# Which queue issues the transfers of the later stages, and three smaller edits, in a four-layer convolution kernel

## The chip, the cores and the metric

The kernel runs on one core of a Trainium2 chip, in one launch. The metric is the device time of that launch in microseconds (us), the median of three runs. A core has five engines that run side by side, each with its own instruction queue that it works through in order: TensorE (PE; its weight loads are shown as PEld), VectorE (DVE), ScalarE (ACT), GpSimd (POOL) and SyncE (SP). Engines wait for each other, and for transfers between memory and the core, by semaphores. A transfer is issued by an instruction in the queue of one engine; the instruction stands in that queue until what it waits for has happened.

## The reference

Four layers follow each other on x with 16 images, 32 channels and 128 x 128 points, each with a normalisation over pairs of channels before it and a residual sum after it:

```python
x = x + _L0_conv_ref(_gn(x), ...)   # a recurrence along the image's columns
x = x + _L1_conv_ref(_gn(x), ...)   # 3x3 sum of absolute differences, quantised
x = x + _L2_conv_ref(_gn(x), ...)   # Hartley transform, 32 x 32 modes mixed, transform back
x = x + _L3_conv_ref(_gn(x), ...)   # five edge operators, then a small encoder and decoder
```

The second layer is the long one. For each image, each output channel f and each point it computes

```python
out[n, f, i, j] = -sum over c, kh, kw of |patch[c, kh, kw] - w[f, c, kh, kw]|
```

with integers in patch and w. The fourth layer has convolutions on 128, 64, 32 and 16 points a side, max pooling between them, and three 2 x 2 deconvolutions back up; its output multiplies its input.

## The kernel before

**First layer** (`stage0`). It runs alone at the start and isn't touched.

**Absolute differences** (`Differences`). The work is cut into 32 units: 16 images by 2 halves of 64 rows. A unit loads its quantised half image once (`loaded`, tile `q`, 128 partitions of 4 channel copies) and makes 72 evaluations, one for each of 8 filter blocks and 9 taps. An evaluation is one instruction over the half image, max(q - w, 0): either on VectorE (L684, tile `d_dve`, three buffers) or on ScalarE (L681, tile `d_act`, two buffers). Each evaluation is summed over the channels by 16 pairs of a weight load and a matmul (`sums`, L586) into four PSUM banks (`acc`); nine `linear` steps add the part of the absolute value that max leaves out. At the end `finish` (L567, L569) adds the residual on VectorE and takes statistics, and stores the rows (L573). Its own transfers are the quantised store (L546), the unit's load (L553), the residual (L560) and the rows to be quantised next (L530).

**Later stages** (`After`). The third and fourth layers run for groups of four images, so there are four groups. Groups 0 to 2 are woven into the units, as soon as their images are finished; group 3 and what is left of group 2 run after the last unit. Before all groups, `prepare` composes weights and stores them in memory (`up`, `fold`). In a group, `forward` loads the images (`xh`, L961), transforms them, stores the modes (`xm_d`, L1010), loads them again in two orders (`xs` and `xw`, L1061) and mixes them with weights (`mix`, L1083; result `z_d`, L1120). `back` loads that (`zi`, L1145), transforms back and adds the residual (`xr`, L1138), and stores x3 (L1188). `frames` loads x3 in strips of rows (`xp`, L1246), which `statistics` (matmuls L1292) and `conv1` (matmuls L1607) read. `small_layers` does the convolutions (L1455) and deconvolutions (`round`, L822 and L847) with `spread` (L1543 on VectorE, L1546 on ScalarE) writing their results, and `last` the final one, with a last store of the output (L1714).

**What sets the order.** Python code plans the order of instructions while the program is built. `Weave` keeps estimated clocks for TensorE, VectorE and ScalarE (`weave.pe`, `weave.dve`, `weave.act`; an evaluation counts 2.36 on VectorE and 7.15 on ScalarE). `Differences.run` asks which engine would finish the next evaluation first, with its buffers taken into account, emits it there, emits sums whose evaluations should be done, and lets `weave.advance` fill in steps of the later stages where TensorE should have room. Steps with `later(us, ...)` are put off by that many planned microseconds: a store comes some us after its computation, a load some us after the store that frees its tile. `keep_order` then ties each engine to this order while the units run. After the last unit `drain` takes turns between two such workers, the rest of group 2 and group 3, each with its own four PSUM banks (`b_ps` and `c_ps`). Nothing on the chip adapts: an instruction that is late holds up what stands behind it on its engine.

Two details matter for the change. A unit's last evaluations were kept from ScalarE, and all its sums were emitted before the next unit's first evaluation:

```python
act = False not in ends or (True in ends and i < 68 and ends[True] <= ends[False] + 0.5)
...
if acc and (not act or i == 71):
    sums(weave.dve, i == 71)
```

And all transfers after the start, of the differences and of the later stages alike, are issued by SyncE (1321 of them; ScalarE issues three at the start, GpSimd none). GpSimd has a few memsets only (L519, L952, L953, L1255) and one reduction.

Of the kernel before, what the change touches and what calls it, by code (L numbers as in the profile page):

```python
# [7 lines left out]
F32 = mybir.dt.float32  # L8
# [8 lines left out]
HW = H * W  # L17
# [282 lines left out]
class Weave:  # L300
# [10 lines left out]
    def __init__(self, work):  # L311
# [3 lines left out]
        self.draining = False  # L315
# [87 lines left out]
def drain(*weaves):  # L403
# [4 lines left out]
    while live:  # L408
# [4 lines left out]
        if us is None:  # L413
            live.remove(w)

# [17 lines left out]
DVE_US, ACT_US, PE_US = 2.36, 7.15, 1.0  # L433
SLACK, CLOCK = 3.0, 1.0
# [3 lines left out]
def rest(nc, tc, cst, sel16, bias, m1, r1, a, d, out):  # L438


    with ExitStack() as ctx:
# [13 lines left out]
        end.side, end.ps = "right", ctx.enter_context(tc.tile_pool(name="c_ps", bufs=4, space=PSUM))  # L455
        end.weave = Weave(end.work([NG - 1]))
# [5 lines left out]
class Differences:  # L462
# [100 lines left out]
    def finish(self, b, half, acc, xr):  # L563
# [46 lines left out]
    def run(self, tc, ctx, weave):  # L610
# [13 lines left out]
        before, following = None, self.loaded(0, 0)  # L624

        free, count = {True: [0.0] * 2, False: [0.0] * 3}, {True: 0, False: 0}
        for b in range(B):
            for half in range(2):
                q, acc = following, None
                late, xq, summed = [], {}, 0  # L630

                def sums(until, last):

                    nonlocal summed
                    while late and (min(late)[0] <= until or last):
                        end, n, act, t = min(late)
                        late.remove((end, n, act, t))
                        self.sums(acc, t, n, not summed, last and not late)
                        summed += 1
                        weave.pe = max(weave.pe, end + 0.2) + PE_US  # L640
                        free[act].append(weave.pe)

                for i in range(72):
                    if not acc and sum(not v[2] for v in late) == 2:

                        if before:
                            self.finish(*before)
                        acc = [ps.tile([128, 512], F32, name="acc1") for _ in range(4)]
                        sums(weave.dve, False)
                    if i % 4 == 0 and 24 <= i < 60:  # L650
                        self.linear(acc, q, i // 4 - 6)
                    if i == 8 and (b, half) != (B - 1, 1):
                        following = self.loaded(b + half, 1 - half)
                    if i == 40:
                        xr = self.residual(b, half)
# [17 lines left out]
                    act = False not in ends or (True in ends and i < 68 and ends[True] <= ends[False] + 0.5)  # L673
# [4 lines left out]
                    late.append((ends[act], i, act, t))  # L678
# [7 lines left out]
                    if acc and (not act or i == 71):  # L686
# [1227 lines left out]
```

## Time and profile before

| | us |
|---|---|
| median of three runs (7311.98 to 7319.36) | 7317.06 |
| the profiled execution | 7308.39 |
| its span, in the trace | 7306.6 |
| TensorE busy | 5566.3 (76%) |
| VectorE busy | 5855.4 (80%) |
| ScalarE busy | 5318.0 (73%) |
| GpSimd busy | 36.3 |
| mean granted clock of TensorE | 0.867 |

The span runs from the first to the last instruction of one execution; the 1.8 us around it are not in the trace. Busy shares over the whole span mix three stages: the first layer up to 920 us, the units up to 5944 us, the drain up to the end. A page of the profile lists groups of instructions by line of the code, with their count, busy time, mean duration in ns, and the idle time of the engine just before them with what ended it. Rows of waits give who waited for whom. SPq is the queue of SyncE: its rows are the issuing instructions and what they waited for.

### The profile page before, as it was taken

The page shows a single profiled execution, that of the slowest core. Times are in us where ns is not written, and L with a number is a line of the kernel's source. Part 1 is how long each engine was busy: PE and PEld are TensorE (multiplying, and loading weights), DVE is VectorE, ACT ScalarE, POOL GpSimd, SP SyncE. Part 2 cuts the span into 40 slices and gives each one's busy share as a digit, 9 for nine tenths or more (in the row PEclk, how much of TensorE's full clock was granted, in tenths as well). Part 3 has the DMA queues.
Part 4 walks back from the last instruction along what each step waited for, and adds up shares of the span by engine and source line. Part 5 has one row for each costly group of instructions (what it writes and reads, how often), then busy time and mean ns, then how long its engine had stood idle before and what let it go on. Part 6 is the DMA issues. An engine that isn't in the chain of part 4 may idle for free. (4 is left out here: it accounts for less than half of the span.)

```text
span 7306.6 us, 258155 instructions
## 1 busy us (share of the span) xinstructions
PE 5566.3 (76%) x121132; PEld 3000.3 (41%) x121132; DVE 5855.4 (80%) x7046; ACT 5318.0 (73%) x3116; POOL 36.3 (0%) x31
## 2 busy tenths in 40 slices
PE   4778566666677687998777676999788777798887
PEld 3665322222244343333344333333334456445544
DVE  7787599999999999999898889999899982423232
ACT  2556399989999998998988878999898941131312
POOL 0000000000000000000000000000000000000000
PEclk9899788888888898998888887999887876799996
DMA  8654111111133442211342243111233245531324
GB/s 312 227 195 164 65 63 55 48 58 51 40 96 106 136 115 78 62 43 50 78 134 94 79 139 111 58 55 50 57 100 100 98 138 151 156 102 46 81 62 96
DMA packets 374268, 721.67 MB, mean 99 GB/s; under 512 B 50896, under 2 KB 219856, under 8 KB 362320
## 3 DMA queue, kind: packets, MB, share of 16 engines
q1 hardware_dynamic: 372768, 704.58, 31.3%
q8 instruction: 948, 15.53, 0.9%
q14 instruction: 120, 0.98, 0.0%
q10 hardware_dynamic: 432, 0.57, 0.0%
HBM read 507.21 MB, written 164.32 MB: 92 GB/s over the span
## 5 line engine op out<-in xcount | busy, mean ns | idle before, releaser
L681 ACT ACTIVATE d_act<-q,neg 128x8192 f16<-128x8192 f16 (+1 forms) x599 | 4237.0, 7141 | 383.8 <-PE acc L586 330.8
L684 DVE TENSOR_SCALAR d_dve<-q,qw 128x8192 f16<-128x8192 f16 (+1 forms) x1705 | 3929.7, 2360 | 187.4 <-PE acc L586 144.1
L586 PE MATMUL acc<-d_dve,sel 128*32 128x512 f16 x27280 | 1957.5, 415 | 750.4 <-DVE d_dve L684 741.5
L586 PEld LDWEIGHTS <-sel 128*32 128x32 f16 x36864 | 1045.7, 103 | 2521.4 <-issue 1862.7
L1607 PE MATMUL acc<-xp,wf 32*32 32x512 f32 x25600 | 1052.9, 625 | 50.7 <-issue 29.9
L586 PE MATMUL acc<-d_act,sel 128*32 128x512 f16 x9584 | 759.4, 439 | 346.2 <-ACT d_act L681 276.9
L1607 PEld LDWEIGHTS acc<-xp,wf 32*32 32x32 f32 x25600 | 415.9, 105 | 428.5 <-issue 344.9
L1252 ACT ACTIVATE xp<-xp,shift,stats 128x1280 f32<-128x1280 f32 (+1 forms) x128 | 182.5, 1434 | 434.5 <-DMA xp<-x_d 298.3
L1546 ACT ACTIVATE y<-pooled,b 32x128 f32<-32x128 f32 x512 | 204.7, 400 | 398.8 <-DVE pooled L1532 392.1
L207 PE MATMUL pg<-h,wb 64*64 64x20 f32 (+15 forms) x4096 | 393.7, 318 | 105.0 <-DVE h L256 64.0
L822 PE MATMUL acc<-y,u_conv 32*32 32x256 f32 (+1 forms) x9728 | 409.9, 491 | 82.6 <-issue 41.0
L244 ACT ACTIVATE gt<-pg,bias 128x20 f32<-128x20 f32 (+15 forms) x1024 | 316.6, 375 | 78.8 <-PE pg L207 72.0
L207 PE MATMUL pg<-e,wb 64*64 64x20 f32 (+15 forms) x4096 | 351.1, 313 | 17.2 <-DVE e L260 6.0
L207 PEld LDWEIGHTS pg<-h,wb 64*64 64x64 f32 x4096 | 245.4, 152 | 140.9 <-DVE h L256 90.5
L207 PE MATMUL pg<-xn,wb 64*64 64x28 f32 (+61 forms) x4096 | 283.9, 302 | 11.6 <-ACT gt L244 3.9
L822 PEld LDWEIGHTS acc<-y,u_conv 32*32 32x32 f32 x9728 | 193.8, 115 | 233.3 <-issue 152.8
L207 PEld LDWEIGHTS pg<-e,wb 64*64 64x64 f32 x4096 | 249.3, 154 | 93.0 <-DVE e L260 63.9
L1292 PE MATMUL acc<-xp 32*64 32x204 f32 (+3 forms) x8576 | 245.6, 351 | 31.5 <-ACT xp L1258 23.4
L255 ACT ACTIVATE th<-c 128x20 f32<-128x20 f32 (+15 forms) x256 | 81.3, 320 | 236.1 <-DVE c L253 234.5
L1735 DVE TENSOR_SCALAR s<-acc,l_ms,l_one 128x512 f32<-128x512 f32 x128 | 102.7, 829 | 168.8 <-PE acc L822 168.8
L207 PEld LDWEIGHTS pg<-xn,wb 64*64 64x64 f32 x4096 | 216.0, 153 | 36.6 <-ACT gt L244 10.9
L1292 PEld LDWEIGHTS acc<-xp 32*64 32x64 f32 (+1 forms) x8576 | 173.3, 137 | 123.5 <-issue 93.3
(203 smaller groups left out, 4173.4 us busy)
## 6 DMA issues: line engine op xcount, KB each, us to landing
xr<-x_d SPq DMA_DIRECT2D x192, 512.0 KB
xp<-x_d SPq DMA_DIRECT2D x112, 640.0 KB
q<-q_d SPq DMA_DIRECT2D x32, 2145.0 KB
x_d<-xr SPq DMA_DIRECT2D x128, 512.0 KB
x_in<-in_x_dram SPq DMA_DIRECT2D x16, 2048.0 KB
res<-in_x_dram SPq DMA_DIRECT2D x64, 512.0 KB
xn<-in_xs_dram SPq DMA_DIRECT2D x64, 512.0 KB
xn<-xn SPq DMA_DIRECT2D x128, 256.0 KB
```

What stands on the lines that cost most here:

```text
L207: nc.tensor.matmul(bank[c][q][64 * pair : 64 * pair + 64, :, :width], wb[half, 4 * kind + KIND[q]].rearrange("p b o -> p (b o)"), v[half], ...
L244: nc.scalar.activation(gt[:, q, :, :n], bank[c][q][:, :, :n], AF.Tanh if q == G else AF.Sigmoid, bias=bias[:, KIND[q] : KIND[q] + 1],)
L255: nc.scalar.activation(th[:, :, :n], cell, AF.Tanh)
L586: self.nc.tensor.matmul(acc[k][32 * j : 32 * j + 32, :], self.sel16[:, i // 9, :], d[:, row : row + 4, c : c + W], start=first, stop=last,)
L681: nc.scalar.activation(dst, src, AF.Relu, bias=self.neg[:, i : i + 1])
L684: nc.vector.tensor_scalar(dst, src, self.qw[:, i : i + 1], 0.0, ALU.subtract, ALU.max)
L822: nc.tensor.matmul(acc[blk][32 * j : 32 * j + 32, o : o + rows * n], t[part, 4 * par + tap, :], src[part, top : top + rows, left : left + ...
L1252: nc.scalar.activation(v, v, AF.Identity, bias=self.shift3, scale=self.stats3[:, 1])
L1292: nc.tensor.matmul(gram[blk][j : j + width, at : at + n], xp[part, l, 2 + j : 2 + j + width], xp[part, rows, j : j + width + 4], start=sta ...
L1546: nc.scalar.activation(d, s, AF.Identity, bias=bj)
L1607: nc.tensor.matmul(acc[blk][32 * j : 32 * j + 32, :], tap_of("all", tap)[rows], xp[rows, 4 * j + kh : 4 * j + kh + 4, kw : kw + W], start= ...
L1735: nc.vector.tensor_scalar(s.rearrange("p r w b -> p b r w"), acc[blk].rearrange("p (b r w) -> p b r w", b=2, w=64), istd[:, blk : blk + 1] ...
```

## The change

- **Transfers.** Every `nc.sync.dma_start` of the later stages becomes `nc.gpsimd.dma_start`: 18 places in `replicated`, `Composed`, `prepare`, `forward`, `modes`, `weights`, `mixing`, `back`, `frames`, `statistics`, `first_layers` and `last`. They are 691 transfers. SyncE keeps those of the first layer and of the absolute differences, 630.
- **ScalarE up to a unit's end.** The rule that keeps it from the last four evaluations goes; from i = 68 on it may end up to the rest of the unit's planned VectorE time and 1.5 more after VectorE. The sums of a unit that are still out are emitted during the next unit's first evaluations, and at the latest just before `finish`, which runs when the next unit has two VectorE evaluations. The state of a unit is now a dictionary.
- **Eight banks for the last group.** When one of the two workers in `drain` has ended, the other is `alone`. From then on it takes its PSUM tiles from both pools in turn, four by four, `spread` alternates between VectorE and ScalarE by block, and a finished output unit is put off by 4 instead of 14 planned microseconds before it is stored.

```diff
         if us is None:
             live.remove(w)
+            for w in live:
+                w.alone = True
...
+LATE = 1.5
...
+        end.spare = bg
...
-        before, following = None, self.loaded(0, 0)
+        following = self.loaded(0, 0)
...
+        def sums(unit, until, last=False):
+
+            late = unit["late"]
+            while late and (min(late)[0] <= until or last):
+                end, n, act, t = min(late)
+                late.remove((end, n, act, t))
+                self.sums(unit["acc"], t, n, unit["summed"] == 0, unit["summed"] == 71)
+                unit["summed"] += 1
+                weave.pe = max(weave.pe, end + 0.2) + PE_US
+                free[act].append(weave.pe)
...
                         if before:
-                            self.finish(*before)
-                        acc = [ps.tile([128, 512], F32, name="acc1") for _ in range(4)]
-                        sums(weave.dve, False)
+                            sums(before, weave.dve, True)
+                            self.finish(**before)
+                        unit["acc"] = [ps.tile([128, 512], F32, name="acc1") for _ in range(4)]
+                        sums(unit, weave.dve)
...
-                    act = False not in ends or (True in ends and i < 68 and ends[True] <= ends[False] + 0.5)
+                    act = False not in ends or (
+                        True in ends and ends[True] <= ends[False] + (0.5 if i < 68 else (71 - i) * DVE_US + LATE)
+                    )
...
-                    if acc and (not act or i == 71):
-                        sums(weave.dve, i == 71)
-                    made = sum(not v[2] for v in late)
-                    if acc:
-                        weave.advance(min([v[0] for v in late] + [weave.dve + DVE_US]))
+                    current = unit if unit["acc"] else before
+                    if current and not act:
+                        sums(current, weave.dve)
+                    due = [v[0] for v in current["late"]] if current else []
+                    if unit["acc"]:
+                        due.append(weave.dve + DVE_US)
                     else:
-                        weave.advance(weave.dve + (2 - made) * DVE_US + (2.6 if before else 0.0))
-                before = b, half, acc, xr
-        self.finish(*before)
+                        made = sum(not v[2] for v in unit["late"])
+                        due.append(weave.dve + (2 - made) * DVE_US + (2.6 if before else 0.0))
+                    weave.advance(min(due))
+                before = unit
+        sums(before, weave.dve, True)
+        self.finish(**before)
...
     def acc(self):
-        return self.ps.tile([128, 512], F32, name="acc")
+
+        self.banks += 1
+        ps = self.spare if self.weave.alone and self.banks // 4 % 2 else self.ps
+        return ps.tile([128, 512], F32, name="acc")
...
-                    nc.sync.dma_start(xh, bass.AP(x2.tensor, first, [[W, H], [HW, 16], [1, W]]))
+                    nc.gpsimd.dma_start(xh, bass.AP(x2.tensor, first, [[W, H], [HW, 16], [1, W]]))
...
-            if engine is nc.vector:
+            if blk % 2 == 0 if weave.alone else engine is nc.vector:
...
-                following[unit] = weave.later(14.0, lambda: store(x, unit))
+                following[unit] = weave.later(4.0 if weave.alone else 14.0, lambda: store(x, unit))
```

The other places where `nc.sync` becomes `nc.gpsimd` have the form of the one shown.

## The prediction

> **What bounds the kernel now.** I read the stretches first, cut where the stages change: the first layer ends at 920 us (first evaluation of a difference, row L684), the differences at 5944 us (last `finish`), and what is left drains to the end. Columns: sum, then busy time (and instructions) of PE, PEld, DVE, ACT and POOL, PE clock, DMA share, GB/s.
>
> ```profile
> 920.00:2176.00 1256.00, 835.30 (x12622) 367.33 (x12625) 1237.39 (x945) 1181.59 (x185) 6.34 (x2) 0.86 0.17 59
> 2176.00:3715.00 1539.00, 1268.32 (x28714) 578.17 (x28710) 1451.47 (x1171) 1430.57 (x470) 2.78 (x4) 0.90 0.29 86
> 3715.00:5467.00 1752.00, 1393.45 (x30238) 654.88 (x30240) 1596.84 (x1293) 1552.38 (x495) 13.03 (x6) 0.88 0.29 86
> 5467.00:5944.00 477.00, 359.15 (x6508) 200.78 (x6501) 451.47 (x332) 424.10 (x64) 6.66 (x3) 0.85 0.28 86
> 5944.00:7306.00 1362.00, 1099.48 (x30758) 725.94 (x30757) 444.53 (x1093) 296.16 (x552) 5.11 (x9) 0.80 0.40 108
> ```
>
> In the differences DVE is busy 4737 of 5024 us: it is the bound, with 287 us idle. ACT is busy 4589, idle 435. The drain is TensorE's, at a granted clock of 0.80. The groups by line show who does the evaluations, the waits by engine (differences only) what the idle time is: us in total, times, longest.
>
> ```profile
> L681 ACT ACTIVATE d_act<-q,neg 128x8192 f16<-128x8192 f16 (+1 forms) x599 | 4237.0, 7141 | 383.8 <-PE acc L586 330.8
> L684 DVE TENSOR_SCALAR d_dve<-q,qw 128x8192 f16<-128x8192 f16 (+1 forms) x1705 | 3929.7, 2360 | 187.4 <-PE acc L586 144.1
> ...
> DVE d_dve L684 <- PE acc L586: 144.1, 88, 26.7
> DVE d_dve L684 <- DMA q<-q_d: 41.2, 1, 41.2
> DVE xr L1182 <- DMA xr<-x_d: 22.6, 1, 22.6
> DVE xm L1004 <- DMA xm_d<-xm: 21.7, 1, 21.7
> DVE xw L1068 <- DMA xw<-xm_d: 16.6, 4, 10.9
> ```
>
> Of DVE's 287 us, 41 are the first load; transfers of the later stages cost 22.6 + 21.7 + 16.6 and, in shorter rows, 8.6 + 8.0 + 5.7 + 2.8, together 86. Why they are late is in the queue of SyncE, which issues all of them in order:
>
> ```profile
> SPq L546 <- DVE qt L543: 1157.1, 52, 46.9
> SPq L573 <- DVE xr L567: 679.6, 57, 87.2
> ...
> 5496.25 63.87 SPq L961 DMA_DIRECT2D xh<-x_d  x6
> ```
>
> Stores of the differences (L546, L573) stand in that queue for up to 87 us, and the later stages' loads behind them. The reverse costs little: ACT waited for `xq` once, 7.5 us.
>
> Last, GpSimd's own timeline (start, us), since it is to issue transfers beside a busy VectorE:
>
> ```profile
> 1564.62 2.47 POOL L952 MEMSET xs<- 64x2048 f32 x1 [709.48 <-DMA fold_d<-fold]
> 1567.14 3.87 POOL L953 MEMSET xs<- 64x2048 f32 x1
> 2334.96 2.21 POOL L1255 MEMSET xp<- 128x132 f32 x1 [763.94 <-DMA zi<-z_d]
> 5961.38 1.80 POOL L953 MEMSET xs<- 64x2048 f32 x1
> 6138.45 0.21 POOL L1255 MEMSET xp<- 128x132 f32 x1 [175.27 <-DVE sides L1322]
> ```
>
> The same memset takes 0.21 us in the drain and 2.21 beside evaluations, the larger one 1.80 and up to 3.87. And the evaluations at 1565.3 and 1569.2 us took 4.005 and 3.970 us, against a mean of 2.360: each side waits for the other's whole instruction, in turn.
>
> **What the Trainium skill says.** "SBUF — State Buffer", section "SBUF: two separate sides": VectorE's two-port modes and GpSimd share one port pair under an exclusive lock for a whole instruction, and a transfer issued by GpSimd, whose descriptors its cores write, starves while VectorE holds it. The memsets above agree for the lock. The same page, "A bandwidth-pool intuition that's wrong": such a transfer grew from about 0.62 to 3.1 us beside a VectorE copy, ending about 0.115 us after it. "DMA: Bandwidth & Descriptors", "Issuing engine by pattern", puts simple loads on SyncE; "Issuing engines are not separate DMA queues" there says that a second issuer saves only the sequencer's time. Here that time is not small, as the queue rows show. No transfer of the kernel before is issued by GpSimd, so the starving itself is not in this trace.
>
> **Part 1, ScalarE to a unit's end.** In the order of instructions of the changed program ScalarE does 625 evaluations instead of 599, VectorE 1679 instead of 1705. VectorE loses 26 x 2.360 = 61 us of its bound; ScalarE gains 26 x 7.141 = 186 us, inside its 435 us idle (331 of them for `d_act` buffers, 61 times: with two buffers and the old rule `i < 68` it rests at each of 32 unit ends). Matmuls stay at 36864. New is that a unit's last sums wait for ScalarE and are made after the next unit's first two VectorE evaluations (4.7 us); `finish` waits for them, and VectorE's next evaluations stand behind `finish`. LATE allows ScalarE to end 1.5 us after VectorE, which leaves some 3 us for 16 matmuls. A late ScalarE (it also does the later stages' work) breaks this now and then: bounds 0 and 2 us x 32 = 64; I take 10. Sum -51. What is late next is ScalarE, with (4589 + 186) / 4950 = 96% busy.
>
> Does the drain give it back? The order says no: behind the last evaluation the same work stands in both programs (6400 matmuls of the first convolution, 2432 of L822, 208 of L1204). The drain's length stays; only the differences shrink.
>
> **Part 2, 691 transfers move to GpSimd's queue, 630 stay on SyncE's.** Gain: no load of a later stage stands behind L546 and L573. Up to the 86 us, and with them the 26.7 us that VectorE waited for TensorE just after the 22.6 us wait for `xr`: 112. GpSimd's queue keeps waits of its own (stores for VectorE, reloads for stores: 224 and 203 us on SyncE's queue now), and each transfer starts later by up to one evaluation, so I take 70. Bounds 0 and 112; below nothing is the slower rival.
>
> Cost on VectorE: a group has 169 transfers, 2.25 groups fall into the differences, with the preparation and the third group's first loads about 420. Each holds the port while descriptors are written, and evaluations are 3930 of 5024 us, 0.8 of the time. Lower bound 0; upper, the page's whole 0.62 us: 420 x 0.62 x 0.8 = 208. I take the 0.115 us that were left after the copy: 420 x 0.115 x 0.8 = 39 (both are estimates from that page). Largest in descriptors are the loads `xh`, 2048 runs of 512 bytes each; SyncE's row shows 64 us for six of them already.
>
> Cost in the drain: nothing else is on the queue there, so nothing is gained; some 15 transfers are on the chain of waits (x_d to xh, zi, v, w_conv 3.94, u_conv 4.49 us, the last store). The skill's "Specifications" of the same DMA page gives about 1 us to the first byte against 0.6; with waiting, 1 us each is my estimate: +15. Bounds 0 and 15 x 2.36 = 35.
>
> **Part 3, the last group alone.** Alone is only the time after group 2's last store, about 7045 to 7306. There the chain has 3.02 us before the second L822 round of `up6` (<-ACT y), about 1 us before each of eight rounds of `last` (<-DVE s, 0.86, 0.93, 0.85) and 1.4 between two rounds of conv2: with four banks more, 12 us can go; the splitting of `spread` over both engines shortens an 11.5 us eviction that the u_conv load partly hides. TensorE's clock there is 0.59 to 0.76[...]. I take -12; bounds 0 and -25.
>
> Sum: -51 - 70 + 39 + 15 - 12 = -79. The profiled execution was 7308.4 us with a span of 7306.6; the runs' median is 7317.1. 7317 - 79 = 7238, rounded 7235.
>
> **The rivals.**
> - The port lock decides: GpSimd holds VectorE for longer than the write, or needs several grants for one transfer. For it: the memsets took 1.65 us from each evaluation they met, and VectorE is the bound. Against: a memset writes a tile, a transfer only descriptors. At 0.62 us a transfer: 7317 - 118 + 208 = 7407. It decides from a hold of 118 / (420 x 0.8) = 0.35 us. If `xh` needs many grants (32 of 2.36 us would be 76 us a load, eight loads a group, where the forward stage now has some 12 us a load), far more.
> - All queue waits go and VectorE's idle time halves, with cheap descriptors: -61 - 112 + 10 - 12 = -175, so 7140. For it: in 920 to 2040 us, where no later stage runs, VectorE waited only 5 us apart from the first load. Against: the planner's lags were counted for SyncE's latency, and slower transfers use them up.
> - Gains and losses cancel: the longer latencies take the 70 back and the hold is somewhat above 0.115 us: 7317 +/- 15.
>
> **How the numbers follow.** Forecast 0.47, all waits gone 0.12, cancel 0.08, lock 0.33. Within the forecast's own range (7170 to 7300) the sign is certain; 0.2% is 15 us, about what can be told from no change. Faster 0.59, same 0.07, slower 0.34. The range takes in the best rival and the lock at 0.62 us: 7110 to 7430; longer stalls of `xh` and a still better case are left out.
>
> **What would show it.** Evaluations by VectorE 1679, still near 2.36 us in the mean (at a 0.115 us hold 2.38; at 0.62 about 2.48); the waits of VectorE for xr, xm, xw transfers gone or short; its waits for TensorE not above 144 us; the differences ending near 5850 us; the drain still about 1362 us. Wrong it is if evaluations of 3 us and more are common, if `xh` or `zi` waits of tens of us appear, or if the drain grows by over 30 us.

## The result and the profile after

The changed kernel takes 7312.94 us (7301.44 to 7317.12, 4 runs) where the kernel before, in the same comparison, takes 7318.21 (7311.98 to 7320.48, 4 runs): ratio 0.9992, interval 0.9974 to 1.0009. No change can be told. The profiled execution has a span of 7309.1 us against 7306.6. The time came out as it did because its parts cancelled: measured one by one in the next section, the transfers cost 85 us, the last group's banks give 49 and ScalarE's evaluations 10. None has the size foretold.

First the stretches of the changed kernel (same columns as before), cut where its last `finish` ends, at 5992 us:

```profile
920.00:5992.00 5072.00, 3847.52 (x78094) 1799.73 (x78093) 4715.39 (x3720) 4772.82 (x1237) 760.05 (x434) 0.88 0.26 79
5992.00:7309.00 1317.00, 1035.74 (x30730) 697.68 (x30730) 440.99 (x1069) 296.18 (x568) 196.74 (x280) 0.82 0.40 111
```

The differences became 48 us longer (5072 us against 5024) and the drain 45 us shorter (1317 against 1362). VectorE lost only 22 us of work in the differences, 4715 against 4737, and its idle time went from 287 to 357 us. ScalarE did its 184 us more.

The page of the changed kernel shows the evaluations, 26 of them moved as planned, and longer by 16 ns each on VectorE:

```profile
L689 ACT ACTIVATE d_act<-q,neg 128x8192 f16<-128x8192 f16 (+1 forms) x625 | 4420.8, 7144 | 242.1 <-PE acc L590 183.8
L692 DVE TENSOR_SCALAR d_dve<-q,qw 128x8192 f16<-128x8192 f16 (+1 forms) x1679 | 3898.2, 2376 | 254.0 <-PE acc L590 210.2
```

Then VectorE's waits in the differences of the changed kernel, total, times and longest:

```profile
DVE d_dve L692 <- PE acc L590: 210.2, 108, 14.3
DVE xw L1084 <- DMA xw<-xm_d: 50.9, 5, 16.2
DVE d_dve L692 <- DMA q<-q_d: 41.6, 1, 41.6
DVE wf L1435 <- DMA v<-fold_d: 22.8, 5, 8.7
...
DVE es_w L1368 <- DMA gm<-in_gram_dram: 5.9, 1, 5.9
DVE xh L999 <- DMA xh<-x_d: 5.3, 1, 5.3
```

The waits for `xr` (22.6 us) and `xm` (21.7) are gone. In their place `xw` and `v` are waited for longer, and VectorE's waits for the later stages' transfers are 50.9 + 22.8 + 5.9 + 5.3 = 85 us, where the kernel before had 86. VectorE's waits for TensorE grew from 144 to 210 us. (The wait for `q` is the first load, in both kernels, and ended before 920 us.)

GpSimd's groups in the differences of the changed kernel (count, busy us, mean ns of an issue):

```profile
L1262 POOL DMA_DIRECT2D xp<-x_d x65 | 128.1, 1974 | 1072.9 <-PE acc L1623 681.6 <-PE acc L1308 190.7 <-PE acc L590 119.0
...
L1693 POOL DMA_DIRECT2D xr<-x_d x32 | 52.0, 1632 | 55.0 <-DMA out_dram<-xr 54.8
L1026 POOL DMA_DIRECT2D xm_d<-xm x24 | 50.5, 2104 | 106.0 <-DVE xm L1020 94.0 <-DVE xw L1084 12.1
```

and the same three lines of code in its drain:

```profile
L1262 POOL DMA_DIRECT2D xp<-x_d x63 | 59.8, 952 | 321.8 <-PE acc L1308 150.0 <-PE acc L1623 139.6 <-issue 13.9
...
L1693 POOL DMA_DIRECT2D xr<-x_d x32 | 17.2, 545 | 24.2 <-DMA out_dram<-xr 20.3 <-DMA u_conv<-up_d 2.8 <-DMA xp<-x_d 1.0
...
L1026 POOL DMA_DIRECT2D xm_d<-xm x8 | 6.3, 798 | 12.6 <-DVE xm L1020 10.3 <-DVE is_t L743 2.0 <-issue 0.4
```

These three issues take 0.5 to 1.0 us in the mean without evaluations and 1.6 to 2.1 us beside them. The difference, 1.0 to 1.3 us, is about half an evaluation: an issue usually waits for what is left of one, once. Single ones wait longer: of the 24 issues of `mix` in the differences two took 34.0 and 34.9 us. This is the starving that the Trainium skill describes in "SBUF — State Buffer", section "SBUF: two separate sides", which the kernel before could not show.

### The profile page after: what moved, and what is told of

Read it like the earlier page. It is cut to its first block, busy times and chain, and to the rows that moved or that the text cites. A ratio compares the mean times of both kernels' runs of the same rounds, so it can differ in the third digit from the quotient of the medians.

```text
span 7309.1 us, 258220 instructions
## 1 busy us (share of the span) xinstructions
PE 5491.0 (75%) x121132; PEld 2967.8 (41%) x121132; DVE 5830.2 (80%) x7004; ACT 5501.6 (75%) x3158; POOL 960.7 (13%) x722
## 4 chain that ended last, share of the span: by engine, by line
PE 25%; issue 16%; DVE 11%; ACT 8%; DMA 7%; POOL 1%; another core or an unknown queue 0%; SPq 0%; DVEq 0%; ACTq 0%; POOLq 0%
PE acc L1623 10%; ACT d_act L689 7%; DVE d_dve L692 6%; PE acc L590 6%; PE acc L834 2%; PE acc L1471 2%; PE acc L1308 2%; DMA v<-fold_d 1%; DMA xp<-x_d 1%; PE acc L1046 1%; DMA xq<-x_d 1%; DMA xm_d<-xm 1%; DMA x_d<-xr 1%; ACT y L1562 1%; DVE y L1559 1%
## 5 line engine op out<-in xcount | busy, mean ns | idle before, releaser
L689 ACT ACTIVATE d_act<-q,neg 128x8192 f16<-128x8192 f16 (+1 forms) x625 | 4420.8, 7144 | 242.1 <-PE acc L590 183.8
L692 DVE TENSOR_SCALAR d_dve<-q,qw 128x8192 f16<-128x8192 f16 (+1 forms) x1679 | 3898.2, 2376 | 254.0 <-PE acc L590 210.2
L1623 PE MATMUL acc<-xp,wf 32*32 32x512 f32 x25600 | 1074.7, 625 | 48.9 <-issue 33.4
L590 PE MATMUL acc<-d_act,sel 128*32 128x512 f16 x10000 | 786.6, 439 | 403.4 <-ACT d_act L689 374.2
L834 PE MATMUL acc<-y,u_conv 32*32 32x256 f32 (+1 forms) x9728 | 344.4, 465 | 71.3 <-issue 51.4
L1262 POOL DMA_DIRECT2D xp<-x_d x128 | 187.9, 1471 | 1394.6 <-PE acc L1623 821.2
L834 PEld LDWEIGHTS acc<-y,u_conv 32*32 32x32 f32 x9728 | 172.0, 111 | 186.9 <-issue 133.4
```

The lines of the kernel that those rows point to most:

```text
L590: self.nc.tensor.matmul(acc[k][32 * j : 32 * j + 32, :], self.sel16[:, i // 9, :], d[:, row : row + 4, c : c + W], start=first, stop=last,)
L689: nc.scalar.activation(dst, src, AF.Relu, bias=self.neg[:, i : i + 1])
L692: nc.vector.tensor_scalar(dst, src, self.qw[:, i : i + 1], 0.0, ALU.subtract, ALU.max)
L834: nc.tensor.matmul(acc[blk][32 * j : 32 * j + 32, o : o + rows * n], t[part, 4 * par + tap, :], src[part, top : top + rows, left : left + ...
L1262: nc.gpsimd.dma_start(v, bc_view(x3, g).rearrange("p (h w) -> p h w", w=W)[:, lo:hi, :])
L1623: nc.tensor.matmul(acc[blk][32 * j : 32 * j + 32, :], tap_of("all", tap)[rows], xp[rows, 4 * j + kh : 4 * j + kh + 4, kw : kw + W], start= ...
```

## The experiments

Times of different comparisons differ by some us, so the ratio against the kernel before, run beside each, is what counts. 0.0014 is 10 us.

| kernel | part 1 | transfers on GpSimd | part 3 | us | ratio, interval |
|---|---|---|---|---|---|
| changed | yes | 691 | yes | 7312.9 | 0.9992 [0.9974, 1.0009] |
| only_scalar | yes | none | no | 7301.0 | 0.9986 [0.9980, 0.9993] |
| only_gpsimd | no | 691 | no | 7386.5 | 1.0116 [1.0099, 1.0134] |
| only_banks | no | none | yes | 7264.3 | 0.9933 [0.9920, 0.9946] |
| all_sync | yes | none | yes | 7257.6 | 0.9932 [0.9917, 0.9946] |
| swapped_b | yes | the differences' 288 | yes | 7391.2 | 1.0132 [1.0111, 1.0153] |
| chain_gpsimd_b | yes | 176, the exchange of modes | yes | 7254.5 | 0.9936 [0.9923, 0.9948] |
| chain_sync_b | yes | 515, all but those | yes | 7283.1 | 0.9965 [0.9952, 0.9977] |
| strips_sync | yes | 563, all but `xp` | yes | 7284.5 | 0.9949 [0.9935, 0.9964] |
| dummy15_b | yes | 480 extra, 128 runs each | yes | 7264.8 | 0.9942 [0.9926, 0.9958] |
| dummy_rows | yes | 480 extra, 2048 runs each | yes | 7457.8 | 1.0196 [1.0182, 1.0210] |
| banks_alone | no | none | banks only | 7276.3 | 0.9942 [0.9929, 0.9954] |
| late_m4 | 615 on ScalarE | none | yes | 7261.9 | 0.9926 [0.9914, 0.9939] |
| act_slack12 | yes, sums 1.2 later | none | yes | 7237.0 | 0.9896 [0.9881, 0.9912] |
| act_slack24 | yes, sums 2.4 later | none | yes | 7186.3 | 0.9828 [0.9812, 0.9844] |
| act_slack36 | yes, sums 3.6 later | none | yes | 7227.4 | 0.9886 [0.9869, 0.9903] |
| old_slack12 | no, sums 1.2 later | none | yes | 7272.7 | 0.9946 [0.9930, 0.9962] |
| old_slack24 | no, sums 2.4 later | none | yes | 7270.0 | 0.9943 [0.9928, 0.9958] |
| gp_slack24 | yes, sums 2.4 later | 691 | yes | 7250.9 | 0.9917 [0.9902, 0.9931] |

### One part at a time

`only_gpsimd`, `only_scalar` and `only_banks` are the kernel before with one part of the change; `all_sync` is the changed kernel with its 18 places put back:

```diff
-                    nc.gpsimd.dma_start(xh, bass.AP(x2.tensor, first, [[W, H], [HW, 16], [1, W]]))
+                    nc.sync.dma_start(xh, bass.AP(x2.tensor, first, [[W, H], [HW, 16], [1, W]]))
```

> The kernel before with the 691 transfers of the later stages on GpSimd's queue and nothing else of the change. If the transfers are what ate the gain (theory A), it is slower than before by 0.6 to 1.5%, 45 to 110 us, nearly all of it in the differences, with VectorE's evaluations near 2.375 us. If ScalarE's evaluations gave nothing (theory B), it is within 0.3% of before: VectorE's lost waits for xr and xm balance the longer ones for xw and wf and 27 us of holding.

> The changed kernel with all transfers back on SyncE, so ScalarE up to a unit's end and eight banks only. Theory A: about 1.2 to 1.5% faster than before (50 us in the drain, 45 to 60 in the differences). Theory B: only the drain's gain, 0.6%, 45 us, with the differences ending at 5944 or later.

> Only ScalarE's evaluations up to a unit's end, all transfers on SyncE, four banks for the last group. Theory A: 0.6 to 0.9% faster, the differences some 50 us shorter. Theory B: within 0.2% of before, since VectorE's 61 us less work come back as waits for TensorE.

> The kernel before with the eight banks for the last group only. Both theories: 0.6% faster, 40 to 50 us, all of it after the last group is alone, the differences unchanged. If it is under 20 us, the drain's gain in the changed kernel came from the other parts.

The transfers alone cost 85 us (1.16% of 7317), and put back they give some 50. So theory A holds for the transfers: they ate what the rest gained. For ScalarE's evaluations theory B holds. `all_sync` gains 0.68% and not 1.2 to 1.5%, and its last `finish` ends at 5955 us, later than the 5944 before. Part 1 alone gives 10 us, and beside part 3 nothing that can be told (0.9932 against 0.9933). Part 3 gives 49 us, as both theories had it once the shorter drain was known; the prediction had 12.

Where this cost arises can be read in the profile of `only_gpsimd`, an execution of 110 us more than the one before. VectorE waits for transfers of the later stages as long as before, 88 us against 86; among them `xr` is still there with 25.4 us. Its evaluations take 31 us more (3960.8 against 3929.7), the drain 16, and its waits for TensorE go from 144 to 192 us. TensorE in turn waits for two loads of the later stages, in the differences of the kernel before:

```profile
PE acc L1096 <- DMA mix<-in_mix_dram: 1.6, 1, 1.6
...
PE acc L1159 <- DMA zi<-z_d: 0.6, 1, 0.6
```

and of `only_gpsimd`:

```profile
PE acc L1096 <- DMA mix<-in_mix_dram: 29.1, 3, 10.5
PE acc L1159 <- DMA zi<-z_d: 24.7, 10, 8.1
```

These 52 us more stand beside the 48 us that VectorE waits more for TensorE. No edit isolates them. But TensorE waits for `zi` in each of the four kernels that have it on GpSimd's queue with most other transfers of the later stages (14.4 us in the changed one, 14.6 to 26.3 in the others), for 0.9 us where it shares that queue with the exchange of modes alone, and less where SyncE issues it (9.6 us in `old_slack24`, 7.6 in `swapped_b`, under 1 in the others).

### Which of GpSimd's transfers cost

`swapped_b` exchanges the queues: the later stages' transfers are issued by SyncE, the 288 of the differences by GpSimd.

```diff
-        self.nc.sync.dma_start(q, bass.AP(q_d.tensor, first, [[0, 4], [(H + 2) * P, C], [1, (self.R + 2) * P]]))
+        self.nc.gpsimd.dma_start(q, bass.AP(q_d.tensor, first, [[0, 4], [(H + 2) * P, C], [1, (self.R + 2) * P]]))
```

> The changed kernel with the queues exchanged: the later stages' transfers on SyncE, those of the absolute differences from unquantised on (xq, q_d, q, xr, x2: 288) on GpSimd. If the queue that both share holds the later stages back and GpSimd's slow issue only hurts where a transfer is on a short chain, it beats the variant with all on SyncE (7258) by 20 to 60 us, since the differences' transfers have a unit's time. If the port lock is what costs, it is slower than that variant by about two thirds of what the change lost against it, some 35 us.

It is 1.32% slower than before and so some 146 us slower than `all_sync`; both theories are missed by far. The DMA issues of this kernel (KB each, median us from issue to landing) show late landings:

```profile
q<-q_d POOLq DMA_DIRECT2D x32, 2145.0 KB, 45.0
...
xr<-x_d POOLq DMA_DIRECT2D x64, 512.0 KB, 26.6
```

The residual `xr` lands 26.6 us after its issue behind a `q` load of 45.0 us; the later stages' `xr` loads, also of 512 KB and on GpSimd's queue, took 7.7 us in the changed kernel. For transfers issued by SyncE the profile gives no such time. And VectorE waits for none of these loads but the first `q`, 58.7 us where `all_sync` has 40.8. What grew is its waits for TensorE, from 188 to 298 us, and ScalarE's for the strips `xp`, which SyncE issues in both, from 24 to 93 us. Which of the moved transfers brings that about stays open. Two queues instead of one are thus no gain by themselves, in either of the two divisions tried.

`chain_gpsimd_b` leaves only the exchange of modes on GpSimd (`xm_d`, `xs`, `xw`, `mix`, `z_d`, `zi`: 176 transfers), `chain_sync_b` puts just these back on SyncE.

> All transfers on SyncE but those of the short chain (xm, xs, xw, mix, z, zi: 176), which GpSimd issues. Latency theory: slower than the variant with all on SyncE by 20 us or more, with VectorE's waits for xw at 50 us. If the shared queue is the worse evil for this chain, it is faster than that variant, by up to 40 us.

> The changed kernel with the transfers of the short chain in the forward stage (xm, xs, xw, mix, z, zi: 176) back on SyncE. Latency theory: half or more of the loss against the variant with all on SyncE goes, 25 to 40 us faster than the change, VectorE's waits for xw gone. Lock theory: the gain is the share of transfers, a quarter, 15 us.

The 176 alone cost nothing (0.9936 against 0.9932 with none), and the evaluations stay at 2.365 us. This holds though VectorE waits 59.5 us for `xw` where `all_sync` has 28.4: such a wait need not cost the kernel its length. The other 515 cost some 24 us (0.9965 against 0.9932), with evaluations at 2.375. The step from 515 to all 691 is another 20 us (0.9992), between what the two theories of `chain_sync_b` had, and its waits for `xw` did not go (29.7 us). So the same 176 transfers cost nothing alone and seem to cost something in a queue with the others; the intervals of 0.9965 and 0.9992 still touch. For the evaluations it is not the count of transfers that matters. `dummy15_b` and `dummy_rows` measure this by itself: to `all_sync` they add 480 transfers issued by GpSimd beside the evaluations, into tiles that nobody reads.

```diff
+                    for n in range(15 * (i + 1) // 72 - 15 * i // 72):
+                        nc.gpsimd.dma_start(self.idle[self.idles % 4], self.idle_src)
+                        self.idles += 1
```

A run is a stretch of bytes that follow each other in memory and in the tile. Each transfer has 128 runs of 64 bytes in `dummy15_b`; in `dummy_rows` the tile is `[:, :, :4]` of 128 x 16 x 5, which makes 2048 runs of 16 bytes, with two such tiles in place of four.

> The variant with all transfers on SyncE, and besides 15 small transfers a unit (480 in all, 128 runs of 64 bytes, into tiles that nobody reads) issued by GpSimd. Nothing waits for them, so their cost is the port alone. Lock theory: it costs most of the 55 us that the change lost against that variant, 40 us or more. Latency theory: only the longer evaluations, 20 to 30 us or less (evaluations' mean up by some 0.015 us), and the rest of the loss comes from transfers that land late.

> The changed kernel with all its own transfers on SyncE (7257.6 us), and 480 extra transfers issued by GpSimd beside the evaluations, each of 2048 runs of 16 bytes into a tile that nobody reads, so that nothing waits for them; nothing is left out. They have 16 times the runs of the small extra transfers tried before (128 runs each), which left the evaluations at 2.364 us and the time 7 us longer. Theory 'it is the number of runs that GpSimd describes that holds VectorE': a later-stage load has 512 to 2048 runs, the mean evaluation on VectorE rises from 2.364 to 2.38 us or more and the time by 30 us or more, to 7285 to 7330. Rival 'the loss is in the latency of the chain of the later stages, not in VectorE's evaluations': nobody waits for these transfers, so the evaluations stay within 2.360 to 2.368 us and the time at 7255 to 7275.

The groups of `dummy15_b`:

```profile
L698 DVE TENSOR_SCALAR d_dve<-q,qw 128x8192 f16<-128x8192 f16 (+1 forms) x1679 | 3875.7, 2364 | 217.4 <-PE acc L590 173.8
...
L653 POOL DMA_DIRECT2D idle<-in_consts_dram x480 | 668.2, 1399 | 1001.9 <-DVE c L251 834.2
```

and of `dummy_rows`:

```profile
L698 DVE TENSOR_SCALAR d_dve<-q,qw 128x8192 f16<-128x8192 f16 (+1 forms) x1679 | 4021.9, 2451 | 204.3 <-PE acc L590 154.7
...
L653 POOL DMA_DIRECT2D idle<-in_consts_dram x480 | 989.6, 2063 | 1701.3 <-DMA idle<-in_consts_dram 846.0
```

480 small transfers left VectorE's evaluations as they were. The same number with 16 times the runs added 4021.9 - 3876.5 = 145 us to them (3876.5 is the sum in `all_sync`), 0.30 us a transfer or 0.15 ns a run. The kernel became about 193 us slower (1.0196 against 0.9932), past the 7330 us at which that theory ended; the 48 us beyond the evaluations are not explained. VectorE's timeline of `dummy_rows` shows single evaluations (start, us):

```profile
1254.19 2.34 DVE L698 TENSOR_SCALAR d_dve<-q,qw 128x8192 f16<-128x8192 f16 x1
...
1256.72 2.66 DVE L698 TENSOR_SCALAR d_dve<-q,qw 128x8192 f16<-128x8192 f16 x1
...
1259.47 2.34 DVE L698 TENSOR_SCALAR d_dve<-q,qw 128x8192 f16<-128x8192 f16 x1
...
1264.36 2.76 DVE L698 TENSOR_SCALAR d_dve<-q,qw 128x8192 f16<-128x8192 f16 x1
```

and GpSimd's of the same stretch:

```profile
1254.63 2.66 POOL L653 DMA_DIRECT2D idle<-in_consts_dram  x1 [0.53 <-DMA idle<-in_consts_dram]
1263.47 1.56 POOL L653 DMA_DIRECT2D idle<-in_consts_dram  x1 [6.18 <-DMA idle<-in_consts_dram]
```

The issue at 1254.63 us starts during an evaluation, which keeps its 2.34 us; it is still under way when the next one starts, and that one takes 2.66. So it is with the issue at 1263.47 and the 2.76 us. The evaluation at 1259.47, with no issue beside it, takes 2.34. In the whole trace the 324 evaluations that start while an issue is under way took 2.82 us in the mean, the other 1355 took 2.36. So an issue waits for the end of one evaluation and then holds up the next. Runs and bytes grew together here (64 bytes a partition against 256), so strictly it is one of the two; the strips below, with 5120 bytes a partition, tell against bytes.

From 0.15 ns a run the cost in the changed kernel can be estimated: in its differences 65 strips `xp` of 1280 runs and 24 `xh` of 2048 make 132,000 runs, 20 us. Measured between `all_sync` and the changed kernel: 3898.2 - 3876.5 = 22 us. By bytes, 0.30 us for 256 bytes a partition would make the 65 strips alone cost 65 x 20 x 0.30 = 390 us. `strips_sync` takes the strips away:

```diff
-            nc.gpsimd.dma_start(v, bc_view(x3, g).rearrange("p (h w) -> p h w", w=W)[:, lo:hi, :])
+            nc.sync.dma_start(v, bc_view(x3, g).rearrange("p (h w) -> p h w", w=W)[:, lo:hi, :])
```

> The changed kernel (7312.9 us) with one kind of transfer put back on SyncE: the 128 loads of the strips xp, 1280 runs of 512 bytes each; the other 563 transfers of the later stages stay on GpSimd. Theory 'loads of many runs lengthen the evaluations': the mean evaluation falls from 2.376 to about 2.366 us, worth 1679 x 0.010 = 17 us, and the time to 7285 to 7297. Rival 'the loss is latency spread over the whole chain of loads and stores': the strips are loaded ahead and seldom waited for, so the time stays at 7303 to 7318.

Its group of evaluations:

```profile
L692 DVE TENSOR_SCALAR d_dve<-q,qw 128x8192 f16<-128x8192 f16 (+1 forms) x1679 | 3886.6, 2370 | 258.9 <-PE acc L590 217.8
```

12 us of evaluations came back, as 65 x 1280 runs at 0.15 ns would have it; the mean fell by 6 ns and not by the 10 expected. The kernel gained about 31 us (0.9949 against 0.9992), just past the fast end of that theory's time. So the strips cost about 20 us in something other than evaluations too. Which wait carries those was not told apart: TensorE's for `zi` is 14.6 us here too.

### Part 1: what takes the 51 us back

In `only_scalar` the stretch of the differences is:

```profile
920.00:5936.00 5016.00, 3823.81 (x78094) 1792.80 (x78093) 4686.83 (x3719) 4769.55 (x1237) 40.49 (x15) 0.88 0.26 80
```

VectorE did 50 us less (4687 against 4737) and stood idle 42 us more (329 against 287). By units: the eighth `finish` began 11.5 us earlier than before (2023.7 against 2035.2), with 14 us of evaluations moved. In the units after it, where later stages are woven in, the lead goes up and down, once to 44 us, and is 8 us at the last `finish`. `late_m4` keeps ScalarE clear of a unit's end by 4 planned us:

```diff
-LATE = 1.5
+LATE = -4.0
```

> The changed kernel with all transfers on SyncE (7257.6 us), and ScalarE allowed to end a unit at most when VectorE's planned end is still 4 us away, instead of up to 1.5 us after it: 615 evaluations on ScalarE, 1689 on VectorE, instead of 625 and 1679. Theory 'a late ScalarE holds the unit's last sums and so takes back what part 1 moves': TensorE's waits for d_act of ScalarE fall and the time is equal or better, 7235 to 7260. Rival 'every evaluation taken from VectorE counts': 10 x 2.36 = 24 us slower, 7270 to 7290.

With ten evaluations more on VectorE the time is the same (0.9926 against 0.9932), and VectorE waited 147 us for TensorE instead of 188. ScalarE's waits for its buffers grew instead, from 187 to 236 us. So here the evaluations alone do not set the time, and the buffers' waits make up the difference. The next kernels leave the evaluations nearly as they are and place the sums of ScalarE's evaluations later in TensorE's order:

```diff
-                    unit["late"].append((ends[act], i, act, t))
+                    unit["late"].append((ends[act] + (2.4 if act else 0.0), i, act, t))
```

`act_slack12`, `act_slack24` and `act_slack36` (1.2, 2.4, 3.6) do it in `all_sync`; `old_slack12` and `old_slack24` in `only_banks`, which has no part 1; `gp_slack24` in the changed kernel itself. The planner reckons from the sums when a buffer is free and when steps of the later stages fit in, so those move too: in `act_slack24` 640 matmuls of the later stages come after the last unit instead of before, and the drain is 1352 us against 1322 in `all_sync`.

> The changed kernel with all its transfers on SyncE (7257.6 us), and the sums of ScalarE's evaluations placed 1.2 planned us later in TensorE's order; 623 evaluations on ScalarE, 1681 on VectorE. Theory 'TensorE stands before a late ScalarE evaluation and so holds VectorE's buffers': TensorE's waits for d_act fall from 364 us by 100 or more, VectorE's waits for TensorE from 188 to 150 or less, and the time to 7210 to 7245. Rival 'the units are held by the later stages' chain of transfers, whatever the order of the sums': the waits for d_act fall and others grow in their place, and the time stays at 7250 to 7275.

> As the last, with 2.4 planned us: about one evaluation of VectorE later; 621 evaluations on ScalarE, 1683 on VectorE. Theory 'TensorE stands before a late ScalarE evaluation': TensorE's waits for d_act are under 200 us, but ScalarE gets its two buffers back later and waits for them more (187 us of it before the change in order); 7205 to 7250. Rival 'the later stages' chain': 7250 to 7290, with ScalarE's waits up and nothing gained.

> The kernel with part 3 only (7264.3 us; no part 1, no part 2), and the sums of ScalarE's evaluations 1.2 planned us later; 594 evaluations on ScalarE, 1710 on VectorE. Theory 'the waits belong to part 1, which fills ScalarE up': here TensorE's waits for d_act are shorter (286 us) and the later sums gain less than in act_slack12, 0 to 15 us. Rival 'they belong to the planner's order whatever ScalarE's share': the same gain as in act_slack12.

> The kernel with part 3 only (7264.3 us), and the sums of ScalarE's evaluations 2.4 planned us later; 598 evaluations on ScalarE, 1706 on VectorE. Theory 'part 1 moves 51 us and TensorE's order took them back': without part 1 the later sums gain little, 7245 to 7280, so that part 1 is worth about 60 us or more once the sums are later (against 7186.3). Rival 'the order was wrong from the start, whatever part 1': 7190 to 7220, and part 1 stays worth under 30 us.

> As act_slack24 (7186.3 us) with 3.6 planned us; 618 evaluations on ScalarE, 1686 on VectorE. Theory: TensorE's waits for d_act fall on, but ScalarE and VectorE get their buffers back later, so the best is near one evaluation of VectorE: 7180 to 7215. Rival 'the later the better': 7120 to 7175.

> The changed kernel as it is (7312.9 us), its later stages' transfers on GpSimd, and the sums of ScalarE's evaluations 2.4 planned us later; 621 evaluations on ScalarE, 1683 on VectorE. Theory 'GpSimd's transfers cost VectorE time and latency in every order of sums': 30 to 70 us above the same with SyncE (7186.3), so 7216 to 7256, evaluations at 2.374 to 2.378 us. Rival 'their cost was the tight order': within 20 us of it, 7180 to 7206.

The waits within the differences of `all_sync`:

```profile
DVE d_dve L692 <- PE acc L590: 188.3, 104, 20.3
...
ACT d_act L689 <- PE acc L590: 187.1, 50, 26.5
```

and of `act_slack24`:

```profile
DVE d_dve L692 <- PE acc L590: 113.0, 73, 8.9
...
ACT d_act L689 <- PE acc L590: 94.9, 37, 17.0
```

Both engines that evaluate wait less for buffers, 208 us together instead of 375, and the kernel is about 76 us faster (0.9828 against 0.9932), the fastest of all: 1.7% below the kernel before, and below what either theory gave. With 1.2 the two waits are 124 + 179 = 303 us, with 3.6 they are 121 + 164 = 286, and the times (7237.0, 7227.4) follow that order; with 3.6 it is slower than the theory had it. One part of the expectation failed: TensorE's own waits for `d_act` were to fall by 100 us and more, and went 368, 391, 347, 300 us. How long TensorE stands before ScalarE's evaluations is therefore not what sets the time; the waits of VectorE and ScalarE for the buffers that it holds are the ones that go with it. Whether the place of the sums does it by itself, or the later stages' steps that move with it, these edits do not separate.

Without part 1 the same edit gains nothing (0.9946 and 0.9943 against 0.9933). With later sums part 1 is worth 84 us (7270.0 to 7186.3), more than the 61 us of evaluations that it moves; with the old order of sums it is worth 10 at most. And GpSimd's transfers cost 64 us with the better order too (7250.9 against 7186.3), with evaluations at 2.375 us: their cost is not a matter of that order.

### Part 3: banks or spread

`banks_alone` has the second set of banks and neither the alternating `spread` nor the earlier store:

```diff
-        return self.ps.tile([128, 512], F32, name="acc")
+        self.banks += 1
+        ps = self.spare if self.weave.alone and self.banks // 4 % 2 else self.ps
+        return ps.tile([128, 512], F32, name="acc")
```

> The kernel before with the eight banks for the last group only; spread stays where the planner puts it and the last output units are stored after 14 planned us as before. The three together took 49 us off. Theory 'TensorE waited for banks': 35 to 50 us faster than before. Rival 'spread on two engines is what counts, since evictions set the pace of the small layers': 0 to 15 us faster, the rest belonging to spread and the earlier store.

The banks alone bring 42 us of the 49, and the 7 that are left for `spread` and the earlier store are within the intervals. The stretch in which the last group is alone (first matmul of L1455 to the last of L822), in the kernel before:

```profile
7067.40:7291.10 223.70, 185.19 (x4386) 108.23 (x4386) 79.51 (x180) 46.06 (x63) 0.00 (x0) 0.69 0.33 75
```

in `banks_alone`:

```profile
7063.00:7248.20 185.20, 135.74 (x4396) 91.95 (x4386) 76.08 (x179) 43.08 (x60) 0.00 (x0) 0.76 0.37 91
```

and in the changed kernel:

```profile
7109.50:7284.50 175.00, 119.35 (x4407) 82.09 (x4386) 74.88 (x160) 43.82 (x76) 18.16 (x33) 0.79 0.40 95
```

The stretch shrinks from 224 to 185 and 175 us. What went is busy time of TensorE, 185 to 136 and 119 us for the same matmuls, not idle time: 38.5 us before, 49.5 with the banks. The groups within the stretch say it by line, first the kernel before:

```profile
L822 PE MATMUL acc<-y,u_conv 32*32 32x256 f32 (+1 forms) x2432 | 139.0, 588 | 27.4 <-issue 16.2 <-DVE s L1735 6.9 <-ACT y L1546 3.0
```

then `banks_alone`:

```profile
L825 PE MATMUL acc<-y,u_conv 32*32 32x256 f32 (+1 forms) x2430 | 96.0, 517 | 40.2 <-issue 33.3 <-DMA u_conv<-up_d 3.8 <-ACT y L1553 3.1
```

The waits for `s` (6.9 us), from which the prediction took its gain, are gone as foretold; they were the small part. The busy time of these 2432 matmuls fell by 43 us, 31%. Other runs agree: with four banks they took 133.7 us (`only_scalar`) and 140.2 (`only_gpsimd`), with eight 83.6 (`all_sync`) and 88.6 (`only_banks`). Their mean duration fell by 12% while the granted clock rose from 0.69 to 0.76; the product of the two is nearly the same, 588 x 0.69 = 406 and 517 x 0.76 = 393. Why the clock rose is not shown. The rest is overlap: 2432 x 588 ns in 139.0 us are 10 matmuls under way at a time, 2430 x 517 ns in 96.0 us are 13, as far as the ends of matmuls, which this profile models, can be trusted.

## Why the prediction was wrong

The forecast of 7235 us was 78 us too fast; the case "Gains and losses cancel", with 0.08, is what happened, though not by its reason alone. Part 2 was put at -70 + 39 + 15 = -16 us and measured +85 alone and some 50 beside the other parts; part 1 at -51 and measured -10; part 3 at -12 and measured -49. That the misses nearly cancel, so that the time did not change, is chance. By its own terms:

**"Sum -51" of part 1 failed.** That VectorE loses 26 x 2.360 us of its bound was right as work: 50 us less in `only_scalar`. The step from work to time was wrong. It took VectorE's idle time in the differences as fixed, except for 10 us of late `finish`; it grew by 42 us, and the part gave 10 us alone and 1 beside part 3. The sentence after it, "What is late next is ScalarE", with 96% busy, named the next limit and priced nothing for it. `act_slack24` and `old_slack24` show what was missing: in the planned order, with ScalarE's sums where they were, the gain is taken back, and with later sums the part brings 84 us.

**"Gain: no load of a later stage stands behind L546 and L573 ... I take 70" failed most.** It took VectorE's waits for transfers to be made by SyncE's queue, and each to be worth its length. With the transfers moved and nothing else (`only_gpsimd`) these waits are 88 us against 86. In the changed kernel the waits for `xr` and `xm` did go, but others took their place, 85 us for 86. And `chain_gpsimd_b` waits 31 us more for `xw` than `all_sync` and takes no longer. What the term left out is TensorE's waits for transfers: with the transfers alone TensorE waited 52 us more for `mix` and `zi`, and VectorE for TensorE 192 us instead of 144, where 26.7 were to go. In the changed kernel that wait rose to 210, part of it with part 1 (166 in `only_scalar`, 188 in `all_sync`). So the term was a loss: of the 110 us by which the profiled execution of `only_gpsimd` is longer, 31 are evaluations, 16 the drain, and 63 are left where the prediction had -70 (by the medians, with 85 in all, 38). Even its bound of nothing was too good. An error of reading belongs here too: the text counted the 41 us of the first load among the 287 us of idle time, though that wait had ended at 920 us; so the idle time not accounted for was larger than it looked. And the rows of SyncE's queue show how long it stood for a result to be stored, up to 87 us; that is not yet time that a second queue saves.

**The hold of the port, "39", was about right in size and wrong in kind.** Evaluations rose by 22 us between `all_sync` and the changed kernel, VectorE's whole busy time by 27.5 (5802.7 to 5830.2); by the page the mean is 2.376 us, where the prediction named 2.38. But it is not 0.115 us a transfer. The lock is seen; a price per transfer, taken over from a single copy, does not carry: 480 small transfers left the evaluations as they were, 480 with 2048 runs cost them 0.30 us each. The fear that `xh` would need many grants was unfounded: its issues took 2.0 us in the mean.

**The drain, "+15".** With the transfers alone it came out: the drain of `only_gpsimd` is 7417.0 - 6038.6 = 1378 us against 1362. In the changed kernel it did not show: the drain is 1317 us, where `all_sync` has 1322. Only the tail behind the last matmul is longer there, 24 us against 15, and 19 of it are there in `banks_alone` too, without GpSimd; some 5 us are left, in which the last store on GpSimd's queue stands.

**"I take -12" of part 3 was mis-sized; measured: 49 us.** The wait that was read is real, but its idle time was taken as all there is to gain. The "bounds 0 and -25" were drawn from idle time too, and the clock there, 0.59 to 0.76, was read as given; its mean over the stretch rose from 0.69 to 0.76. Too few banks showed here as matmuls that overlap less as well, 10 at a time instead of 13.

**Net.** -10, +85 and -49 of the three parts alone make +26; together they made -5 (7318.2 to 7312.9). So GpSimd's transfers cost less beside the other parts: 85 us alone, about 48 on top of them, 64 with later sums. That their latencies fall into waits that part 1 brings anyway is a reading: TensorE's waits for `mix` are 22 us with part 1 alone, 29 with the transfers alone, and 21 with both. No edit isolates it. Of the tests that the prediction named, the mean evaluation and the waits for `xr` and `xm` came out as it said. The waits for `xw` (50.9 us instead of 16.6), VectorE's for TensorE, the end of the differences (5992 instead of 5850) and the drain (1317 us instead of 1362, by part 3) did not. A sign of being wrong that it named, `zi` waits of tens of us, is in `only_gpsimd`, on TensorE and as a sum of ten waits.

The advice of "DMA: Bandwidth & Descriptors", section "Issuing engine by pattern" (simple loads on SyncE), holds here, with some 50 us between the two; the prediction argued past it with the long waits in SyncE's queue, but with the transfers on a queue of their own VectorE waited for them as long as before.

## What to carry to other kernels

- Here work taken from the bounding engine was worth its duration only when the engine behind it followed. Where a third engine consumes both engines' results in a planned order, move that order along with the work, or test it by one edit of the order.
- Before a transfer is moved to GpSimd beside a VectorE that is busy in such evaluations, count its runs and not the transfers: here putting the strips of 1280 runs back on SyncE gained 31 us, and 480 small transfers left VectorE's evaluations as they were.
- Ask of every engine what it waits for in a queue that is to move. Here the bounding engine's own waits for transfers stayed as long as they were, and TensorE's, which hold its buffers, grew.
- Too few banks showed here less as idle time than as matmuls that overlap little: compare a stage's busy time per matmul with that of a stage that has enough, before its gain is read off the gaps.

## What was not expected of the hardware

- 480 transfers of 128 runs, issued by GpSimd beside VectorE's evaluations, left their mean at 2.364 us; as many of 2048 runs raised it to 2.451. The issue itself took 1.40 and 2.06 us. An issue waited for the end of one evaluation and held up the next: those that started with an issue under way took 2.82 us, the others 2.36.
- A 2145 KB load issued by GpSimd landed after 45.0 us, and 512 KB loads in the same queue after 26.6, where 512 KB loads of the later stages on GpSimd's queue took 7.7. What they take from SyncE's queue the profile does not show.
- TensorE's busy time for the same 2432 matmuls was 139.0 us with four banks and 96.0 with eight. At the same number of clock cycles the granted clock (0.69 and 0.76) would cover 139.0 x (1 - 0.69 / 0.76) = 13 of these 43 us, an estimate; the rest is more matmuls under way at a time.
